# Batch 1's transposes on TensorE, a shorter scale chain and a new instruction order in a fused cross-attention and mixture-of-experts kernel

## The chip, the cores and the metric

The kernel runs on one core of one Trainium2 chip. The metric is device time in microseconds (us), from launch to the last output. The profile adds one recorded execution, whose span runs from its first to its last instruction.

## The reference

There are 8 batches of 512 rows with 256 features (`x`), each with a context of 512 rows of 512 features and a mask of 512 entries. All arithmetic is float32.

```python
# per batch
n   = layernorm(x)                                   # 512 x 256
kv  = (ctx @ W_src.T + b_src) * mask[:, None]        # keys 256, values 256
q   = (n @ W_tgt.T + b_tgt) * mask[:, None]
att = softmax(q k.T / sqrt(32), masked)              # 8 heads of 32
x   = x + concat(n, att @ v) @ W_out.T + b_out
f   = layernorm(x)
w   = top 8 of 16 sigmoid scores of l2norm(f) @ l2norm(gate_w).T, normalized
x   = x + sum_e w[e] * (silu(f @ w_gate[e]) * (f @ w_up[e])) @ w_down[e] + shared expert
```

All 16 experts and the shared one are computed for every row, and a row's 8 unused weights are zero. An expert has a hidden width of 128.

## The kernel before

**Arithmetic.** TensorE multiplies in f16. Every float32 operand is split into a high and a low f16 part, and each product takes three matmuls (`mm3`). ScalarE writes the high part and VectorE or GpSimd the low part by a subtraction. So that the parts keep their digits, operands are scaled by powers of two. For a context that power is found at run time: `attention` takes sums of squares (`junk`, into `cs`), TensorE turns the row maxima (`csT`), a `chain` of VectorE instructions on one element makes the power and its inverse from the exponent's bits, and TensorE spreads both over the partitions (`csB`).

**Stages of a batch.** `attention(b)` loads context, mask and `x`, splits and transposes the context (`ch`) and the normalized `x` (`xh`), projects keys, queries and values (`k`, `q`, `v`), and then runs eight score tiles. A tile covers 4 heads, 128 rows and 512 columns and fills one PSUM buffer, of which there is one (`S=1`). It goes through scores `s` on TensorE, the maximum `nm` on VectorE, four exponentials `p32` on ScalarE, and in two halves through the split `pn` (ScalarE, then GpSimd), a DMA transpose into `pt`, and the product `o` on TensorE. The heads' outputs `on` are transposed (`oh`), projected (`oo`) and added to `x`, once for each half of the batch. `route` normalizes that `x` a second time (`xf`), transposes it (`f`), takes router logits (`lg`) and writes the expert weights to DRAM (`cd`), from where a broadcast load (`cb`) brings each expert's. `ffn` runs 17 experts: `g` and `u` on TensorE, elementwise work on the other three engines, and `y`, in groups of 5, 4, 4 and 4 experts. Batch 0 is routed in two halves, so its `g` and `u` have 256 columns; all others have 512.

**The transposes.** For batch 0, `ctx`, `x`, `o` and the second `x` are transposed on TensorE against the identity into PSUM, as float32, and split from there by ScalarE and VectorE. From batch 1 on, `turn` splits first (names `xm`, `om`, `fm`: ScalarE the high part, GpSimd the low one for `xm` and `om`, VectorE for `fm`) and issues two DMA transposes of 32 tiles each on SyncE's queue; `ch` is done the same way in `cn` with four of 64 tiles. Every `pt` is one of 128 tiles. All other loads and stores are on that queue, too.

**The order.** Nothing is written in a fixed order by hand. `record` lists every operation with a due time `vt`: `attention(b+1)` lies about one batch ahead of `ffn(b)`. `schedule` then plays the list through a table of durations, engine by engine, and emits instructions in the order of the planned starts. Among operations that could start first it takes the one with the lowest due time, no further than `AHEAD` past the oldest open one. `RANK` shifts the due time of each kind of operation and stage by a constant. `SLOTS` says how many buffers each kind of tile has. An engine runs its instructions strictly in that order, so one that waits holds up all that stand behind it.

Of the kernel before, what the change touches and what calls it, by code (L numbers as in the profile page):

```python
# [9 lines left out]
F32 = mybir.dt.float32  # L10
F16 = mybir.dt.float16
# [8 lines left out]
P = 128  # L20
# [11 lines left out]
    x=2, n2=5, cx=4, c16=2, ch=1, xh=1, f=2, qk=4, row=2, mb=1, mx=2, mt=1, p32=2, pn=2, pp=3, v3=2, oc=2, oh=2,  # L32
    cb=3, act=5, hx=6, W=NE + 1, cd=2, mr=1,
# [97 lines left out]
class Plan:  # L131
# [5 lines left out]
    def add(self, eng, dur, calls, port=False, size=0, after=()):  # L137
        outs, ins = [], list(after)
        for _, out, args, kw in calls:
            outs += [o for o in (*out, kw.get("accum_out")) if is_view(o)]  # L140
            ins += [a for a in (*args, *(v for k, v in kw.items() if k != "accum_out")) if is_view(a)]
        name = (outs[0] if isinstance(outs[0], Buf) else outs[0].buf).name
        tag = "".join(c for c in name if not c.isdigit()).strip("_") + eng
        vt = self.vt + RANK.get(tag, {}).get(STAGE.get(self.batch, 2), 0.0)
        op = Op(eng, dur, calls, outs, ins, vt, len(self.ops), port, size)
        op.tag = (self.batch, tag)
        self.ops.append(op)
        return op
# [45 lines left out]
    def dmat(self, tiles, out, in_):  # L194
        self.add("SP", max(1240.0, 16.4 * tiles), [self.call("sync.dma_start_transpose", out, in_)], size=4000 * tiles)

    def dma(self, size, out, in_):
        self.add("SP", 360.0, [self.call("sync.dma_start", out, in_)], size=size)


AHEAD = 1.366
RANK = {
    "aACT": {0: 0.1537, 1: 0.0033, 2: -0.4983, 7: 0.1955},
    "aDVE": {0: 0.0254, 1: 0.2498, 2: -0.2428},
    "aPOOL": {0: -0.0113, 1: 0.6968, 2: 0.5586, 7: 0.0013},
    "amaPE": {-1: 0.2806},
    "ambPE": {-1: 0.1166},
    "bobDVE": {-1: 0.5078},
    "bobSP": {-1: -0.2061},
    "bvbDVE": {-1: 0.105},  # L210
    "cTPE": {0: 0.5508},
    "cbSP": {0: 0.2177, 2: 0.7056, 7: 0.5622},
    "cdSP": {0: 0.0041, 1: -0.029, 2: 0.2104},
    "chACT": {0: -0.6068},
    "chDVE": {0: 0.2153},
    "chSP": {1: 0.0075, 2: -0.8976, 7: -1.0876},
    "cnACT": {1: -0.6307, 2: -0.7293, 7: -0.9914},
    "cnDVE": {1: 0.0087, 2: -0.0023, 7: 0.0346},
    "colsSP": {-1: -0.0672},
    "csBPE": {2: -0.1535, 7: -0.0124},  # L220
    "csTPE": {0: -0.1204, 1: -0.0287, 2: -1.2814, 7: -0.0309},
    "ctACT": {0: 0.864, 1: 0.1003, 2: 0.7227, 7: -0.1018},
    "cxPOOL": {0: 0.6459},
    "cxSP": {-1: 0.0735, 1: 0.0526, 2: -0.9286, 7: -0.0609},
    "fACT": {0: 0.0039},
    "fDVE": {0: 1.0851},
    "fSP": {1: 0.3396, 2: -0.0242, 7: 0.4824},
    "fTPE": {0: 0.3035},
    "fmACT": {1: 0.3782, 2: -0.0974, 7: -0.0187},
    "fmDVE": {2: 0.5311, 7: -0.0959},  # L230
    "fmPE": {-1: -0.1267},
    "fmaPE": {-1: 0.1564},
    "fmbPE": {-1: -0.4319},
    "gPE": {0: 0.1235, 1: 0.207, 2: 0.1559, 7: 0.6056},
    "gTPE": {0: 0.3676, 1: 0.5965, 2: -0.1162, 7: -0.0034},
    "gsqDVE": {-1: -0.4317},
    "gw_nDVE": {-1: -0.1543},
    "gw_nSP": {-1: -2.0117},
    "gwsACT": {-1: 0.0234},
    "gwsDVE": {-1: 0.6316},  # L240
    "hACT": {0: -0.6213, 1: 0.3291, 2: -0.1853, 7: -0.0131},
    "hDVE": {0: 0.1408, 1: 0.0071, 2: -0.2515, 7: -0.0144},
    "hPOOL": {0: -0.3695, 1: 0.2141, 2: -0.0944, 7: 0.3346},
    "junkACT": {1: -0.0113, 2: -0.018, 7: 0.0007},
    "kACT": {0: 0.3565, 1: -0.9183, 2: -0.1216},
    "kDVE": {0: 0.4038, 1: 0.1818, 2: -0.0333, 7: 0.0991},
    "kPE": {0: -0.2174, 1: -0.0614, 2: -0.0344, 7: -1.3012},
    "lgPE": {0: 0.2761, 1: -0.3919, 2: -0.2135, 7: 0.0154},
    "mbSP": {-1: -0.7576, 1: 0.96, 2: 0.035, 7: 0.1462},
    "mcolDVE": {-1: -0.5544},  # L250
    "mkSP": {-1: -0.0456},
    "mkTPE": {-1: -0.2494},
    "mrDVE": {0: 0.88, 1: 0.1094, 2: 0.5668},
    "mvDVE": {0: 0.3115, 1: 0.2223, 2: 0.1576, 7: -0.6709},
    "mwDVE": {1: -0.5933, 2: 0.5831, 7: -0.1328},
    "nmACT": {0: 0.3158, 1: -0.251, 2: -0.0551, 7: -0.0427},
    "nmDVE": {0: 0.0026, 1: 0.0593, 2: -0.1259, 7: -0.1155},
    "oPE": {0: 0.0273, 1: -0.0232, 2: 0.0553, 7: 0.0423},
    "oTPE": {0: 0.1833},
    "ocACT": {0: 0.1024, 1: 0.1925, 2: 0.2005, 7: 0.4061},  # L260
    "ocDVE": {0: 0.1704, 1: -0.1219, 2: -0.6326, 7: -0.0917},
    "ohACT": {0: 0.4072},
    "ohDVE": {0: -0.1733},
    "ohSP": {1: 0.1129, 2: -0.0398, 7: -0.3174},
    "omACT": {2: 0.2922, 7: 0.0002},
    "omPOOL": {1: -0.0603, 2: -0.0508, 7: 0.7467},
    "onPOOL": {0: 0.7499, 1: -0.853, 2: -0.1829, 7: -0.2491},
    "onesPOOL": {-1: -0.3119},
    "ooPE": {0: 0.4931, 1: -0.4365, 2: -0.6844, 7: -0.4352},
    "outSP": {0: 0.4027, 1: -0.3028, 2: 0.4122, 7: 0.4538},  # L270
    "pACT": {0: 0.0182, 1: -0.6748, 2: -0.0234},
    "pnACT": {0: 0.2152, 1: 0.2561, 2: 0.1906, 7: 0.0196},
    "pnPOOL": {0: 0.1635, 1: 0.0141, 2: 0.2234},
    "ptSP": {0: 0.4655, 1: -0.4384, 2: 0.1266, 7: 0.3368},
    "qACT": {0: 0.1257, 1: -0.3375, 2: -0.3996, 7: -0.129},
    "qDVE": {0: -0.2704, 1: -0.4202, 2: -0.5367, 7: -0.2649},
    "qPE": {0: -0.3731, 1: -0.0506, 2: -0.194, 7: -1.1345},
    "qPOOL": {0: -0.0185, 1: 0.126, 7: -0.8731},
    "rDVE": {0: -0.1233, 1: -0.1058, 2: 0.0001, 7: -0.3334},
    "rawSP": {-1: -0.1474},  # L280
    "rhPOOL": {0: -0.1646, 1: -0.4627, 2: 0.6826, 7: 0.2987},
    "riDVE": {0: -0.198, 1: 0.6361, 2: 0.1284, 7: -0.0834},
    "sPE": {1: 0.0314, 2: -0.3686, 7: -0.8384},
    "scACT": {0: -0.0831, 1: 0.4518, 2: -0.1934, 7: -0.1498},
    "scDVE": {0: 0.3459, 1: -0.1583, 2: 0.1869, 7: -0.186},
    "scPOOL": {0: -0.0709, 1: 0.1093, 2: -0.1766, 7: 0.0205},
    "smallDVE": {-1: 0.3026, 1: -0.1537, 2: -0.254, 7: -0.5587},
    "smallPOOL": {-1: -0.2347, 0: -0.1282, 1: -0.3163, 2: 0.0089, 7: 0.0576},
    "sqwACT": {-1: -0.5218},
    "sqwPOOL": {-1: -0.1816},  # L290
    "tDVE": {0: 0.0006, 1: -0.5031, 2: 0.36, 7: 0.0922},
    "uDVE": {0: 0.1229, 1: 0.634, 2: -0.239, 7: -0.259},
    "uPE": {0: -0.1486, 1: 0.6035, 2: 0.715},
    "vACT": {0: 0.2058, 1: 0.1873, 2: -0.0086, 7: 0.1161},
    "vDVE": {0: 0.3577, 1: 0.1322, 2: -0.9791, 7: -0.0565},
    "vPE": {0: 1.1408, 1: -1.3367, 2: -0.1245, 7: 0.2457},
    "vPOOL": {0: -0.0824, 1: -0.3013, 2: -0.4353, 7: 0.59},
    "veDVE": {0: 0.124, 1: -0.0703, 2: -0.0253, 7: -1.3962},
    "vfDVE": {0: 0.0546, 1: -0.7051, 2: 0.0069, 7: 0.2438},
    "wACT": {-1: -0.1553},  # L300
    "wDVE": {-1: -0.0168},
    "wmaPE": {-1: -0.2382},
    "wmbPE": {-1: -0.7302},
    "woACT": {-1: -0.6539},
    "woDVE": {-1: 0.1164},
    "woTPE": {-1: 0.5609},
    "wo_nSP": {-1: 0.2082},
    "wsACT": {-1: -0.3273},
    "wsDVE": {-1: -0.0925},
    "wsTPE": {-1: 0.9299},  # L310
    "ws_naSP": {-1: -0.9149},
    "ws_nbSP": {-1: 0.0231},
    "wtACT": {-1: 0.4585},
    "wtDVE": {-1: 0.4299},
    "wtTPE": {-1: -0.4778},
    "wt_nSP": {-1: 0.0823},
    "xDVE": {0: 0.124, 1: 0.2257, 2: -0.3319, 7: 0.1379},
    "xPOOL": {0: -0.0121, 1: 0.02, 2: 0.1123, 7: -0.199},
    "xSP": {0: 1.1008, 1: 0.0058, 2: 0.0641, 7: 0.353},
    "xTPE": {0: 0.4516},  # L320
    "xfACT": {0: -0.1806, 1: 0.1451, 2: -0.1422, 7: -0.437},
    "xhDVE": {0: 0.6081},
    "xhSP": {1: 0.2024, 2: -0.7682, 7: 0.2589},
    "xmACT": {1: 0.1813, 2: 0.1954},
    "xmPOOL": {1: -0.0234, 2: 0.0256, 7: 0.0077},
    "xnACT": {0: 0.0363, 1: -0.1228, 2: 0.2161, 7: -0.0338},
    "xnSP": {-1: -4.4201, 1: -0.3353, 2: -0.0611, 7: -0.0009},
    "xoPE": {0: -0.2204, 1: -0.0378, 2: -0.3262, 7: -0.1335},
    "yPE": {0: 0.3541, 2: 0.148, 7: 0.1762},
# [7 lines left out]
SAME = {"PE": 0.0, "ACT": 20.0, "DVE": 20.0, "POOL": 20.0}  # L337


def schedule(ops):  # L340
# [9 lines left out]
    port = 0.0  # L350

# [33 lines left out]
    while done < len(ops):  # L385
# [21 lines left out]
        op.start, op.end = st, st + op.dur  # L407
# [694 lines left out]
```

## Time and profile before

| | us |
|---|---|
| median of 3 runs | 959.8 |
| the runs | 959.8, 959.16, 963.09 |
| profiled execution, time | 962.42 |
| profiled execution, span | 960.3 |
| TensorE busy | 860.6 (90%) |
| VectorE, ScalarE, GpSimd busy | 668.5, 654.2, 680.4 |
| mean granted TensorE clock | 0.972 |

The profiled execution is 2.6 us over the median, and 2.1 us of its time lie outside the span. The page gives busy time by engine, then a strip of 40 slices of 24 us, then groups of instructions with the idle time just before them and what ended it. The names in a group are the tile names above without their numbers. Nearly all instructions come from one line, so they are told apart by tile.

### The profile page before, as it was taken

What the parts mean: (1) busy time and instruction counts of PE and PEld (TensorE: products, weight loads), DVE (VectorE), ACT (ScalarE), POOL (GpSimd) and SP (SyncE); (2) the same over time, 40 slices, a digit from 0 to 9 for tenths busy, and PEclk for the clock granted to TensorE, in tenths of its full rate; (3) what the DMA queues carried; (4) which work ended last, traced back from release to release, by engine and by line L of the source; (5) the groups of instructions that cost most, each with busy time, mean ns of one, the idle gap of its engine ahead of it and who ended that gap; (6) DMA issues with size and microseconds to landing.
All of it is one profiled execution on the core that took longest, in us unless ns stands there. A gap on an engine that the chain in (4) does not pass through costs nothing.

```text
span 960.3 us, 21139 instructions
## 1 busy us (share of the span) xinstructions
PE 860.6 (90%) x8007; PEld 547.0 (57%) x8007; DVE 668.5 (70%) x1311; ACT 654.2 (68%) x1133; POOL 680.4 (71%) x830
## 2 busy tenths in 40 slices
PE   3874768989789998989999999989999999999997
PEld 2452446766555565636655556646555666565655
DVE  6666778855876677757785688757886687567554
ACT  3588887874877687757786587757787777534231
POOL 4577778876768787677858786787848976853432
PEclk9886999999889999999999999999999999999999
DMA  8868787798699967999599977998499968951411
GB/s 254 271 124 175 138 157 130 151 197 162 121 205 184 201 133 139 211 191 178 104 198 182 197 145 137 204 191 181 88 189 197 178 110 144 214 120 26 123 56 44
DMA packets 395542, 152.43 MB, mean 159 GB/s; under 512 B 347008, under 2 KB 375216, under 8 KB 395440
## 3 DMA queue, kind: packets, MB, share of 16 engines
q1 hardware_dynamic: 395440, 151.08, 77.9%
q8 instruction: 63, 1.03, 0.5%
q14 instruction: 39, 0.32, 0.2%
HBM read 61.12 MB, written 4.46 MB: 68 GB/s over the span
## 4 chain that ended last, share of the span: by engine, by line
PE 55%; DMA 12%; ACT 11%; DVE 8%; POOL 5%; issue 3%; SPq 1%; POOLq 0%; ACTq 0%; DVEq 0%
PE y L1071 14%; PE u L1071 13%; PE g L1071 12%; DMA pt<-pn 8%; PE s L1071 4%; ACT p L1071 3%; PE o L1071 3%; POOL pn L1071 3%; PE v L1071 3%; DVE nm L1071 3%; PE k L1071 2%; ACT pn L1071 2%; DMA cb<-cd 2%; PE oo L1071 2%; SPq L1071 1%
## 5 line engine op out<-in xcount | busy, mean ns | idle before, releaser
L1071 POOL TENSOR_TENSOR pn<-p,pn 128x1024 f16<-128x1024 f32 x128 | 274.6, 2151 | 57.8 <-ACT pn L1071 48.7
L1071 PEld LDWEIGHTS <-w 128*128 128x128 f16 x1836 | 172.1, 98 | 172.1 <-issue 19.3
L1071 POOL TENSOR_TENSOR a<-a,cb 128x512 f32<-128x512 f32 (+1 forms) x144 | 166.1, 1165 | 73.5 <-DVE a L1071 34.6
L1071 ACT ACTIVATE p<-s,nm,small 128x512 f32<-128x512 f32 x256 | 192.3, 782 | 10.6 <-POOL pn L1071 8.1
L1071 PE MATMUL g<-f,w 128*128 128x512 f16 (+1 forms) x918 | 194.7, 357 | 3.7 <-DVE oc L1071 1.3
L1071 PE MATMUL u<-f,w 128*128 128x512 f16 (+1 forms) x918 | 194.1, 358 | 1.6 <-DVE a L1071 1.6
L1071 PE MATMUL y<-w,h 128*128 128x256 f16 x1632 | 185.9, 273 | 5.6 <-DVE h L1071 4.1
L1071 PEld LDWEIGHTS <-h 128*128 128x128 f16 x1632 | 158.5, 98 | 32.0 <-DVE h L1071 6.7
L1071 ACT CAST pn<-p 128x1024 f16<-128x1024 f32 x128 | 134.5, 1053 | 60.8 <-DMA pt<-pn 60.7
L1071 DVE TENSOR_REDUCE nm<-s 128x4 f32<-128x2048 f32 x64 | 146.2, 2285 | 14.7 <-PE s L1071 14.6
L1071 ACT ACTIVATE a<-g,small 128x512 f32<-128x512 f32 (+1 forms) x153 | 98.1, 645 | 51.7 <-PE g L1071 49.8
L1071 DVE SCALAR_TENSOR_TENSOR a<-a,g 128x512 f32<-128x512 f32 (+1 forms) x153 | 94.5, 622 | 39.1 <-ACT a L1071 38.0
L1071 ACT CAST h<-u 128x512 f16<-128x512 f32 (+1 forms) x117 | 62.8, 540 | 51.0 <-DVE u L1071 49.2
L1071 PEld LDWEIGHTS <-pt 128*128 128x128 f16 x2048 | 69.8, 97 | 36.8 <-DMA pt<-pn 16.5
L1071 DVE TENSOR_TENSOR h<-u,h 128x512 f16<-128x512 f32 (+1 forms) x117 | 72.6, 625 | 25.7 <-ACT h L1071 24.1
L1071 DVE SCALAR_TENSOR_TENSOR x<-y,small,x 128x512 f32<-128x512 f32 x64 | 47.8, 748 | 60.9 <-PE y L1071 60.6
L1071 DVE TENSOR_TENSOR u<-u,a 128x512 f32<-128x512 f32 (+1 forms) x108 | 68.4, 635 | 27.5 <-PE u L1071 22.7
L1071 PE MATMUL o<-v,pt 128*128 128x65 f16 (+1 forms) x2048 | 74.2, 187 | 13.5 <-DMA pt<-pn 10.9
L1071 PE MATMUL s<-k,q 32*128 32x512 f16 x768 | 56.1, 396 | 21.2 <-ACT p L1071 20.7
L1071 POOL TENSOR_TENSOR on<-oc,r 128x128 f32<-128x128 f32 x64 | 30.1, 472 | 31.9 <-DVE oc L1071 20.1
L1071 POOL TENSOR_TENSOR h<-a,h 128x512 f16<-128x512 f32 (+1 forms) x36 | 40.3, 1120 | 15.2 <-ACT h L1071 14.9
L1071 PE MATMUL k<-ch,ws 128*128 128x512 f16 x192 | 45.6, 390 | 5.4 <-DMA ch<-cn 4.1
(188 smaller groups left out, 1055.8 us busy)
## 6 DMA issues: line engine op xcount, KB each, us to landing
cb<-cd SPq DMA_DIRECT2D x112, 256.0 KB, 3.9
cx<-in_ctx_dram SPq DMA_DIRECT2D x32, 256.0 KB, 3.6
xn<-in_x_dram SPq DMA_DIRECT2D x16, 256.0 KB, 3.4
x<-in_x_dram SPq DMA_DIRECT2D x8, 512.0 KB, 4.3
cb<-cd SPq DMA_DIRECT2D x32, 128.0 KB, 3.5
out_dram<-x SPq DMA_DIRECT2D x16, 256.0 KB, 3.1
mb<-in_mask_BxS_fk_dram SPq DMA_DIRECT2D x8, 256.0 KB, 4.6
raw<-in_L_ffn_w_gate_dram SPq DMA_DIRECT2D x16, 128.0 KB, 3.3
```

Source lines behind the costliest of these rows:

```text
L1071: getattr(getattr(nc, eng), m)(*[real(v) for v in (*out, *args_)], **{k: real(v) for k, v in kw.items()})
```

## The change

- `x`, `o` and the second `x` of batch 1 are transposed on TensorE, as those of batch 0 are; `turn` serves them from batch 2 on. The context of batch 1 stays with the DMA transposes. In `route`, the transposes now cover four chunks of rows (two `xf` tiles).
- The chain for a context's scale has four instructions after the reduction in place of seven. One multiply and one lower bound move into the constant `cf2`.
- The planner's model: a DMA transpose is charged 6137 bytes a tile at 272 bytes/ns instead of 4000 at 250 and starts its transfer at its own lead; later DMA issues are held back behind transposes; TensorE work is stretched to twice its length where a model of its clock says so (`Clock`). `AHEAD` and every entry of `RANK` have new values.
- Buffers: `pn` and `oc` have three instead of two, `act` six instead of five, `row` and `oh` one instead of two, `W` 17 instead of 18. The last expert's raw weights are loaded into a `pn` buffer for their squares, and a second time into a `pn` buffer when they are split.

```diff
-    x=2, n2=5, cx=4, c16=2, ch=1, xh=1, f=2, qk=4, row=2, mb=1, mx=2, mt=1, p32=2, pn=2, pp=3, v3=2, oc=2, oh=2,
-    cb=3, act=5, hx=6, W=NE + 1, cd=2, mr=1,
+    x=2, n2=5, cx=4, c16=2, ch=1, xh=1, f=2, qk=4, row=1, mb=1, mx=2, mt=1, p32=2, pn=3, pp=3, v3=2, oc=3, oh=1,
+    cb=3, act=6, hx=6, W=NE, cd=2, mr=1,
...
     def dmat(self, tiles, out, in_):
-        self.add("SP", max(1240.0, 16.4 * tiles), [...], size=4000 * tiles)
+        self.add("SP", max(1240.0, 16.4 * tiles), [...], size=6137 * tiles, lead=650.0 - 4.7 * tiles)
...
-AHEAD = 1.366
+AHEAD = 1.42618182031
 RANK = {
...
+HALFWIN, COLD, HOT = 1706.5, 0.49, 0.82
+class Clock:
+    def run(self, t, work):
+        while True:
+            while self.w < int(t / HALFWIN):
+                f = (self.busy + self.before) / (2 * HALFWIN)
+                self.cold = f <= HOT if self.cold else f < COLD
+                self.before, self.busy = self.busy, 0.0
+                self.w += 1
+            end, r = (self.w + 1) * HALFWIN, 2.0 if self.cold else 1.0
...
-        op.start, op.end = st, st + op.dur
+        op.start, op.end = st, clock.run(st, op.dur) if e == "PE" else st + op.dur
...
         if e == "SP":
-            dma_free = max(dma_free, op.end + 900.0) + op.size / 250.0
+            dma_free = max(dma_free, st + op.lead) + op.size / 272.0
             op.end = dma_free
+            if op.lead < 950.0:
+                free[e] = max(free[e], dma_free - 900.0)
...
+        raw = raws[e] = load_raw(e, "W" if n + 1 < NE else "pn")
...
+        if n + 1 == NE:
+            raw = load_raw(e, "pn")
...
-        chain = [tt(f2[:, 0:1], f2[:, 0:1], cf2[:1], ALU.max),
-                 ts(ex[:, 0:1], ex[:, 0:1], 23, None, ALU.logical_shift_right), ts(ex[:, 0:1], ex[:, 0:1], 20, 125, ALU.max, ALU.add),
-                 ts(ex[:, 0:1], ex[:, 0:1], 1, None, ALU.logical_shift_right), ts(ex[:, 1:2], ex[:, 0:1], 3, None, ALU.subtract),
-                 ts(ex[:, 0:1], ex[:, 0:1], -1, 257, ALU.mult, ALU.add), ts(ex, ex, 23, None, ALU.logical_shift_left)]
+        chain = [stt(f2[:, 0:1], f2[:, 0:1], 2.0, cf2[:1], ALU.mult, ALU.max),
+                 ts(ex[:, 0:1], ex[:, 0:1], 24, 23, ALU.logical_shift_right, ALU.logical_shift_left),
+                 ts(ex[:, 1:2], ex[:, 0:1], 1, 59 << 23, ALU.mult, ALU.add), ts(ex[:, 0:1], ex[:, 0:1], -1, 195 << 23, ALU.mult, ALU.add)]
...
         for k in range(2):
-            if b == 0:
+            if b < 2:
                 t = ps(f"xT{b}{k}")
...
-            if b:
+            if b > 1:
                 turn(on, oh, 0, f"om{b}{hf}", p.pool)
...
-            if b:
+            if b > 1:
                 turn(xf, f, c, f"fm{b}{c}")
-        for k in range(0 if b else 2):
+        for k in range(0 if b > 1 else 2):
             t = ps(f"fT{i}{k}")
-            p.pe(*[p.tr(..., xf[:, c, k * P : (k + 1) * P], ident) for c in range(n)], after=[f[:, :, k, :]])
+            p.pe(*[p.tr(..., xfs[c // 2][:, c % 2, k * P : (k + 1) * P], ident) for c in range(n)], after=[f[:, :, k, :]])
```

## The prediction

> **What bounds the kernel.** I read the strip of 40 slices first, and then the table of busy time by stretches.
>
> ```profile
> span 960.3 us, 21139 instructions
> PE   3874768989789998989999999989999999999997
> PEclk9886999999889999999999999999999999999999
> DMA  8868787798699967999599977998499968951411
> ```
>
> ```profile
> 48.00:72.00 24.00, 18.70 (x244) 13.35 (x241) 16.07 (x48) 19.92 (x33) 18.76 (x16) 0.82 0.67 124
> 72.00:96.00 24.00, 10.09 (x121) 6.65 (x122) 14.96 (x17) 19.98 (x31) 18.21 (x26) 0.64 0.85 175
> 240.00:264.00 24.00, 18.02 (x220) 13.16 (x218) 19.35 (x45) 20.44 (x39) 17.77 (x30) 0.87 0.66 120
> 264.00:288.00 24.00, 20.55 (x199) 12.06 (x199) 16.93 (x44) 18.46 (x33) 16.69 (x29) 0.84 1.08 206
> 576.00:600.00 24.00, 23.16 (x215) 15.51 (x212) 20.47 (x43) 17.70 (x31) 15.22 (x28) 1.00 0.70 134
> ```
>
> The second column is TensorE's busy time, the third last its granted clock. After 336 us TensorE is busy and at full clock almost throughout; before that it waits, and then runs slowly too (0.64 to 0.87). ScalarE is the busiest engine at 72 to 96 us.
>
> To place the loss I use a lag: the time at which a score tile starts, less the TensorE work that stands ahead of it in the order at full clock. The rates are from steady rows: 12 `u` matmuls of 512 columns in 2.60 us (0.217 each), 48 `y` matmuls of 256 columns in 5.24 (0.109), one score tile 0.97, 16 `o` matmuls 0.44, one transpose 0.11. The lag is 26.1 us at the first tile, 64.6 at batch 1's first, 81.0 at its fifth and 82.5 at its last, 89.5 at batch 2's first, 90.1 and 103.7 at its third and fifth, 107.8 at batch 3's first and 135.8 at the last of all. All TensorE work sums to 818 us. Of some 142 us lost, 108 lie before 325 us. The chain of waits and TensorE's timeline show what makes up the middle:
>
> ```profile
> 205.70 7.04 DMA ch<-cn
> 212.79 4.45 PE k L1071 x12
> ...
> 264.12 3.62 DMA f<-fm
> 267.79 0.33 PE lg L1071 x6
> 268.11 2.57 PE g L1071 x6
> ```
>
> ```profile
> 257.87 0.57 PE L1071 MATMUL csB<-small,ones 1*128 1x2 f32 x2 [2.80 <-DVE small L1071]
> 259.77 1.47 PE L1071 MATMUL s<-k,q 32*128 32x512 f16 x12 [1.32 <-ACT p L1071]
> 263.45 0.33 PE L1071 MATMUL lg<-gws,f 128*128 128x16 f16 x6 [0.20 <-DMA f<-fm]
> 267.27 0.33 PE L1071 MATMUL lg<-gws,f 128*128 128x16 f16 x6 [3.49 <-DMA f<-fm]
> ```
>
> A bracket is idle time and who ended it. TensorE waits for batch 1's `f` through the DMA queue, for batch 2's scale, and for batch 2's `ch`; after each wait matmuls take twice as long (12 of 512 columns 4.45 us, 6 take 2.57).
>
> **Part by part**, against the profiled execution's 962.4 us.
>
> *f of batch 1.* The four SyncE transposes and the `fm` step go; two groups of four TensorE transposes and a split from PSUM come. Its waits cost 0.20 + 3.49 + 0.18 = 3.9 us and the slow clock behind them 2.57 - 1.30 and, in `xo`, 1.81 - 1.31: 5.6 in all. In the new order 12.1 us of TensorE work lie between batch 1's last `oo` and `lg` (10.5 before). The last `xf` ended 11.9 us after that `oo`; then come transposes 0.44, cast 0.59, subtraction 0.69 and again some of these, about 2.5. The chain of 14.4 leaves a wait of 2.3. Gain 3.3; bounds 0 and 5.6.
>
> *The scale chain.* Before, one two-input instruction (0.53 us) and six one-input ones (1.03); now one and three: 0.5 less per batch, and only where TensorE waits for it. For batch 3, 4.0 us of work now stand between `csT` and `csB`, where 0.4 did; the chain took 3.5 (254.37 to 257.87). The wait of 2.80, the 1.32 behind it, and the slow score tile (1.92 for 0.97) go: gain 5.1. For batch 2 the work between falls from 2.9 to 0.4, and a chain of 3.0 shows: cost 2.0. The other batches have 2.6 or more and stay at nothing.
>
> *ch of batch 2.* Before, its last DMA transpose was issued behind `pt` tiles that fill SyncE's queue, and `k` waited 2.47 us and ran 4.45 - 2.60 = 1.85 too long. In the new order all four stand ahead of a `pt` whose `o` comes before that `k` on TensorE, so that `k` has nothing of its own to wait for. Gain 4.3; bounds 0 (the wait moves to that `o`) and 7.0, the lag's growth there.
>
> *FFN work drawn ahead.* Up to batch 1's fifth tile ScalarE sets the pace (21.4 us busy in 96 to 120). By mean rows its work ahead of that tile is 134.4 us now and 132.7 before; TensorE's is 94.8 and 87.1. If ScalarE keeps its pace, 7.7 - 1.7 = 6.0 us of lag are gone; bounds 0 and 10.
>
> *Transposes and their cover.* 24 of 0.11 us: 2.6 on TensorE, 5.2 at half clock. Four subtractions of 1.16 us leave GpSimd; `xh` and `oh` add four of 0.69 to VectorE, and `f` saves two of 0.25, 2.3 us that its idle time hides (3.8 of 24 us at 144 to 168); with that gone they cost 2.3. SyncE loses 12 issues of 1.24 to 1.67 us, 15 to 20 us of queue, which stood before the `pt` of batch 0's late tiles and of batch 2's first. Beyond `f` and `ch` I take 1.5, between 0 and 3.
>
> [...] The transposes of `pt` hold SyncE's queue 2.97 us for 512 KB each when it is full (221.43 and 228.63 us), 177 GB/s, while plain loads filled the second slice with 271. [...] On the other side, TensorE's transposes of `oT` at 142 us start 0.11 apart. [...]
>
> *Edits at nothing.* The second load of one expert (three issues of 0.43 us on SyncE, beside batch 0's first `cb`) hides behind the wait of GpSimd's `a`; uncovered it is 1.3. The third `pn` buffer answers the largest wait of ScalarE:
>
> ```profile
> L1071 ACT CAST pn<-p 128x1024 f16<-128x1024 f32 x128 | 134.5, 1053 | 60.8 <-DMA pt<-pn 60.7
> ```
>
> But 60.1 of it lie after 170 us, where TensorE has other work; its own waits for `pt` after 336 us sum to 10.3. Nothing, bound 10 gained. One `row` and one `oh` buffer: TensorE holds their next writers apart by several matmul groups; nothing, bound 3 lost. The start does source weights and `v` first: 18.5 us of TensorE work stand before the first score tile (13.8 before), but 25.9 and 24.6 before the third, so it evens out; bounds 6 lost and 4 gained. Batches 3 to 7, where the lag grows by 28.0 us: nothing taken, bounds below.
>
> Sum: 3.3 + 5.1 - 2.0 + 4.3 + 6.0 - 2.6 + 1.5 = 15.6 us. 962.4 - 15.6 = 946.8 in a profiled execution, and 2.6 less in the median: 944.
>
> **Rivals.**
>
> *Slower: the router waits in the later batches.* For batches 3, 4, 5 and 7 the TensorE work between the last `oo` and `lg` falls from 28.7, 28.7, 30.0 and 22.2 us to 15.1, 15.1, 14.9 and 13.0, and these keep their DMA transposes.
>
> ```profile
> 350.87 1.47 PE L1071 MATMUL oo<-wo,oh 128*128 128x256 f16 x12
> 361.51 2.06 ACT L1071 ACTIVATE xf<-x,small,vf 128x256 f32<-128x256 f32 x4
> 369.30 5.68 SPq L1071 DMA_TRANSPOSE f<-fm  x4
> 377.44 0.75 PE L1071 MATMUL lg<-gws,f 128*128 128x16 f16 x24
> ```
>
> In batch 2 that took 25.1 us (352.3 to 377.4). For it: TensorE would stall in order, with everything behind `lg`. Against it: only about 16 are needed in a row (6.9 to the bias, by 352.4 to 358.7 and two GpSimd steps; 1.1 first `xf` pair, 1.5 split, 5.0 of issue, 1.3 landing), and the rest was queueing behind work with nearer use. At 16 the four stalls sum to 6; at 18.5 they come to 16 and take back the whole gain, from where it is slower; at 25 they cost 42. Time 960 to 986. Chance 0.17.
>
> *No change: the front is paced elsewhere.* ScalarE's work before batch 2's fifth tile is 207.1 us after and 208.1 before. If attention arrives no sooner and FFN work doesn't fill its gaps, only the scale's and `ch`'s waits go, and the transposes are paid: 959.8 - 5.1 + 2.0 - 4.3 + 2.6 = 955, with 2 to 5 more if `o` takes over the wait for `ch`. 954 to 961. Chance 0.13.
>
> *More: the third `pn` and less queueing carry on.* The waits for `pt` after 336 us (10.3) and half of the lag's other growth there go too: 944 - 12 = 932, range 922 to 934. Chance 0.17.
>
> **How the numbers follow.** The forecast has 0.53, with 934 to 954 as its own range. The range of 924 to 966 leaves out a little of the top case and about half of the slow one. A measurement of this kernel tells 0.5% from no change, 955.0 to 964.6. Faster: 0.53 + 0.17 + 0.04 of the no-change case = 0.74. Same: 0.09 + 0.02 of the slow one's low end = 0.11. Slower: 0.15.
>
> **What would show it.** Right: no wait of `lg` over 3 us at batch 1, `csB` of batch 3 and `k` of batch 2 without idle time ahead of them, clock slices near 264 us at 9, and a lag of about 75 at batch 1's fifth tile and 88 at batch 2's fifth. Wrong: a wait at `lg` of 4 us or more in batches 3 to 5, a first score tile after 46 us, or lag growing by more than 28 from batch 3 on.

## The result and the profile after

The changed kernel took 967.5 us (median of 6 runs, 965.4 to 968.7) beside 960.7 for the kernel before (6 runs). The ratio is 1.0062, 95% interval 1.0041 to 1.0084: slower by 0.6%. The forecast was 944. The profiled execution took 965.4, its span 963.7.

The strip of the page of after:

```profile
span 963.7 us, 21105 instructions
...
PE   3944878899899999999899998999998999998997
...
PEclk8956899899999999999999999999999999999999
DMA  8868667798698968996599947997699839982411
```

Slices 11 and 12 (241 to 289 us) went from 7 and 8 to 8 and 9 and their clock from 8 to 9, as forecast. But the third slice fell from 7 to 4, and from 458 us on four slices stand at 8 where one did. The table of busy time by stretches of after (TensorE's busy time second, granted clock third from the end):

```profile
48.00:72.00 24.00, 10.84 (x176) 6.94 (x175) 11.68 (x21) 19.83 (x35) 20.86 (x13) 0.58 0.62 132
72.00:96.00 24.00, 9.65 (x126) 6.22 (x127) 17.01 (x30) 16.74 (x25) 14.91 (x29) 0.64 0.85 154
240.00:264.00 24.00, 20.88 (x250) 16.15 (x249) 19.00 (x47) 21.30 (x42) 18.59 (x30) 1.00 0.61 130
264.00:288.00 24.00, 22.32 (x220) 12.94 (x219) 18.78 (x44) 19.80 (x35) 16.51 (x22) 0.93 0.99 184
576.00:600.00 24.00, 19.78 (x202) 11.88 (x199) 18.21 (x49) 19.88 (x37) 12.38 (x16) 1.00 0.69 138
```

ScalarE, which was to keep its pace at the start, is busy 16.74 us of 24 at 72 to 96 us where it was 19.98, and TensorE at 576 to 600 us lost 3.4 us. The three waits on which the forecast's gain rested are gone, as TensorE's timeline of after shows:

```profile
213.25 2.75 PE L1110 MATMUL k<-ch,ws 128*128 128x512 f16 x12
...
261.71 0.28 PE L1110 MATMUL csB<-small,ones 1*128 1x2 f32 x2
...
265.33 0.23 PE L1110 MATMUL lg<-gws,f 128*128 128x16 f16 x3 [0.97 <-DVE f L1110]
265.93 0.68 PE L1110 MATMUL lg<-gws,f 128*128 128x16 f16 x21 [0.36 <-DVE f L1110]
```

The lag, counted as in the prediction, says where it was lost. Its growth in each stretch, in us, with two kernels told of below (n_before and n_after, two of those in the next table):

| stretch | before | forecast | after | n_before | n_after |
|---|---|---|---|---|---|
| start to batch 0's fourth tile | 38.8 | 38.8 | 38.6 | 39.7 | 37.9 |
| to batch 1's fifth tile | 42.2 | 36.2 | 49.5 | 45.6 | 44.6 |
| to batch 3's first | 26.8 | 16.1 | 14.3 | 24.8 | 10.7 |
| to batch 7's last | 28.0 | 28.0 | 31.9 | 20.1 | 15.6 |
| to the end | 6.6 | 6.6 | 8.9 | 5.1 | 6.1 |
| TensorE's work | 817.9 | 820.5 | 820.5 | 817.9 | 820.5 |
| span | 960.3 | 944.7 | 963.7 | 953.2 | 935.4 |

(The forecast's column leaves 1.5 us for SyncE unplaced, which stands in its span.) The middle came out better than forecast. The second stretch missed by 13.3 us and the last two by 6.2.

### The profile page after: what moved, and what is told of

Same layout as the page of the kernel before. It is cut to its first block, busy times and chain, and to the rows that moved or that the text cites. A ratio compares the mean times of both kernels' runs of the same rounds, so it can differ in the third digit from the quotient of the medians.

```text
span 963.7 us, 21105 instructions
## 1 busy us (share of the span) xinstructions
PE 863.9 (90%) x8031; PEld 550.1 (57%) x8031; DVE 676.8 (70%) x1292; ACT 652.1 (68%) x1133; POOL 667.2 (69%) x826
## 4 chain that ended last, share of the span: by engine, by line
PE 51%; ACT 12%; DMA 12%; POOL 10%; DVE 10%; issue 5%; SPq 1%; ACTq 0%; POOLq 0%; DVEq 0%
PE y L1110 12%; PE u L1110 11%; PE g L1110 10%; DMA pt<-pn 5%; ACT p L1110 4%; POOL pn L1110 4%; PE s L1110 4%; PE o L1110 3%; DVE nm L1110 3%; PE v L1110 3%; PE k L1110 2%; POOL a L1110 2%; ACT pn L1110 2%; PE oo L1110 2%; PE xo L1110 1%
## 5 line engine op out<-in xcount | busy, mean ns | idle before, releaser
L1110 PE MATMUL g<-f,w 128*128 128x512 f16 (+1 forms) x918 | 198.9, 360 | 7.2 <-DVE h L1110 3.6
L1110 PE MATMUL y<-w,h 128*128 128x256 f16 x1632 | 190.0, 275 | 4.9 <-DVE h L1110 4.6
L1110 DVE SCALAR_TENSOR_TENSOR a<-a,g 128x512 f32<-128x512 f32 (+1 forms) x153 | 94.1, 622 | 42.7 <-ACT a L1110 42.2
L1110 PE MATMUL o<-v,pt 128*128 128x65 f16 (+1 forms) x2048 | 77.7, 188 | 24.6 <-DMA pt<-pn 22.8
L1110 ACT ACTIVATE nm<-nm,small 128x4 f32<-128x4 f32 x64 | 24.8, 388 | 64.3 <-DVE nm L1110 63.9
L1110 POOL TENSOR_TENSOR h<-a,h 128x512 f16<-128x512 f32 (+1 forms) x36 | 38.6, 1072 | 21.3 <-ACT h L1110 21.3
L1110 PE MATMUL v<-ws,ch 128*128 128x256 f16 x384 | 46.5, 280 | 0.3 <-DVE a L1110 0.3
```

The costliest lines, as they stand in the source:

```text
L1110: getattr(getattr(nc, eng), m)(*[real(v) for v in (*out, *args_)], **{k: real(v) for k, v in kw.items()})
```

## Two theories

*Theory 1:* the edits gain what they were made for, and the new order of instructions, that is the values of `AHEAD` and `RANK`, eats it. *Theory 2:* the edits themselves cost (TensorE's transposes with their splits, one `W`, `row` and `oh` buffer less), in any order.

Two kinds of kernels tell them apart. Some keep an order and change the code: the planner plans with one kernel's operations, and those of the variant are then emitted in that sequence.

```diff
-    ops = schedule(record(io))
+    ops = pinned(record, io)    # sequence from schedule() with the first code, operations from the second
```

The others get other values of `AHEAD` and `RANK` for the code, from a search that minimizes the planner's own planned end. Each kernel ran beside the kernel before, whose median lay between 960.2 and 963.6 us from one series to the next, so kernels are to be compared by the ratios.

| kernel | code | order | us | ratio to before, interval |
|---|---|---|---|---|
| b_pin | before | before | 963.4 | 0.9999 (0.9976 to 1.0022) |
| b_newchain | + short chain | before | 958.5 | 0.9953 (0.9933 to 0.9973) |
| b_tr | + transposes | before | 962.4 | 1.0011 (0.9991 to 1.0030) |
| b_both | + both | before | 959.6 | 0.9954 (0.9931 to 0.9976) |
| a_pin | after | after | 968.3 | 1.0076 (1.0050 to 1.0101) |
| a_oldchain | - short chain | after | 969.2 | 1.0074 (1.0051 to 1.0096) |
| a_notr | - transposes | after | 987.2 | 1.0252 (1.0225 to 1.0279) |
| n_before | before, new planner | searched | 953.8 | 0.9922 (0.9897 to 0.9947) |
| n_oldplan | after, old planner | searched | 968.5 | 1.0074 (1.0044 to 1.0104) |
| n_after2 | after | searched | 960.0 | 0.9977 (0.9956 to 0.9997) |
| n_after | after | searched | 938.5 | 0.9766 (0.9740 to 0.9793) |
| n_pin | after | that of n_after | 943.0 | 0.9786 (0.9756 to 0.9816) |
| n_oldchain | - short chain | that of n_after | 948.3 | 0.9848 (0.9815 to 0.9881) |

## Experiments: the edits in a kept order

Emitting in a kept sequence deals equal buffers out afresh, so the unchanged kernels were run in this form too, as b_pin and a_pin.

> The kernel before, every instruction in its own order; only which of equal buffers (PSUM banks, act) a tile gets is dealt out afresh, as in the runs with one edit. Theory 1 (the short chain is what gained in b_newchain): ratio 0.998 to 1.002. Rival (the dealing of banks gained it): 0.993 to 0.997.

> The changed kernel, every instruction in its own order; only which of equal buffers (pn, act) a tile gets is dealt out afresh. All theories: as the changed kernel, ratio to before 1.004 to 1.008; what it differs by is the price of that dealing, and is taken off the runs made in the same way.

b_pin is level with before and a_pin lies with the changed kernel. The dealing is no cause that these runs can tell.

**The short chain in the old order.** b_newchain is before's order with the four instructions of the change's diff.

> The kernel before with its own order, but the scale's chain of four instructions instead of seven. Theory 1: 0.5 us less in each batch and TensorE waited for it 9.9 us in six, so 1 to 3 us faster, ratio 0.997 to 0.999, the wait of csB in batch 2 about 2.3 instead of 2.80. Theory 2: no gain, ratio 1.000.

It was faster by 0.5%, some 4 us and more than expected. The wait of 2.80 us fell to 2.27, but all waits of TensorE's matmuls at `csB` for VectorE fell only from 4.8 to 3.5 us (the 9.9 us in the expectation count the idle time of the weight loads too). Where the rest arises was not traced. The wait of 2.80 is batch 3's; the expectation and the prediction's opening call it batch 2's, the prediction's sum has it right.

**The transposes in the old order.** In b_tr `b == 0` becomes `b < 2` in the three places of the diff; the added steps stand directly behind what they read.

> The kernel before with its own order of every instruction, but batch 1's x, o and second x transposed on TensorE as in the change (the steps that this adds stand directly behind what they read). Theory 1 (the edits gain, the new order eats it): faster than before by 4 to 10 us, ratio 0.990 to 0.996; the lag's growth from batch 2's first score tile to its fifth falls from 13.6 (89.5 to 103.7, less 0.6) to about 7, and lg of batch 1 waits under 1 us. Theory 2 (the edits themselves cost): 962 or more, ratio 1.000 to 1.006, with the lag at batch 2's fifth tile still over 100 us.

A miss: no difference. The local part came, smaller than expected (the lag's growth from batch 2's first score tile to its fifth, 14.2 before, was 10.0, and the lag at batch 3's first tile 103.0 for 107.8), but 2.6 us of TensorE work were added and 2.3 us of the gain were given back by batch 7.

> The kernel before with its own order, with both edits at once: batch 1's x, o and second x transposed on TensorE, and the scale's chain of four instructions. Theory 1 (the edits gain what the two runs alone showed, and the new order is what eats it): about the sum of the two ratios, 0.994 to 0.998, so 955 to 958 us, with the lag at batch 3's first score tile about 101 (107.8 before, 103.0 and 105.1 with one edit each). Theory 2 (the edits take the gain from each other): 0.999 to 1.003.

Both together gave what the chain gave alone. In the old order the two edits are worth 0.5% and cost nothing, which speaks against theory 2. The buffers are those of before in these kernels, and no run changes them alone.

**The edits taken out of the new order.**

```diff
-        chain = [stt(f2...), ts(ex...), ts(ex...), ts(ex...)]          # a_oldchain
+        chain = [tt(f2...), ts(ex...), ts(ex...), ts(ex...), ts(ex...), ts(ex...), ts(ex...)]
-            if b > 1: turn(on, oh, ...)                                # a_notr; likewise xh and f
+            if b: turn(on, oh, ...)
```

> The changed kernel with its own order, but the old chain of seven instructions. Theory 1 (the place in the order decides, not the chain's length): the csB waits of 3.31 us in batches 5 and 6 grow by about 0.5 each, and the whole by 1 to 4 us: ratio to before 1.007 to 1.010. Theory 2 (the short chain itself costs): at or below the changed kernel, 1.003 to 1.006.

> The changed kernel with its own order, but batch 1's x, o and second x transposed by SyncE's DMAs again as before (the steps that come back stand directly behind what they read). Theory 1: the waits return, of lg of batch 1 by 4 to 8 us and at xo and oo of batch 1, less 2.6 us of TensorE's transposes: 3 to 10 us slower than the changed kernel, ratio to before 1.009 to 1.017. Theory 2 (the transposes themselves are the cost): 0.998 to 1.004.

The waits of 3.31 us at `csB` in batches 5 and 6 grew to 3.86, as expected, but the time by less than could be told: a_oldchain is level with a_pin. The DMA transposes cost 1.7% against a_pin (1.0252 to 1.0076, some 17 us), more than expected. TensorE's timeline of a_notr:

```profile
275.40 0.33 PE L1192 MATMUL lg<-gws,f 128*128 128x16 f16 x6 [3.53 <-DMA f<-fm]
...
280.44 0.33 PE L1192 MATMUL lg<-gws,f 128*128 128x16 f16 x6 [3.45 <-DMA f<-fm]
```

Between 184 and 340 us TensorE's waits of `lg` for `f` sum to 8.9 us and those of `oo` for `oh` to 4.8. The rest was not traced, and a part may be the place of the steps that came back, put by hand into an order laid out without them. As placed here, the transposes are worth nothing in the one order and 1.7% in the other: what an edit is worth belongs to the order.

## Experiments: another order for the same edits

```diff
-AHEAD = 1.42618182031
+AHEAD = 1.621858
...
-    "csBPE": {0: 0.4147, 1: 0.0276, 2: -0.453, 7: -0.0822},
-    "csTPE": {0: 0.712, 1: 0.012, 7: 0.4638},
+    "csBPE": {0: 0.7807, 1: -1.3106, 2: -1.4906, 7: -0.938},
+    "csTPE": {0: -0.6625, 1: -1.0967, 2: -0.7041, 7: -0.652},
```

(n_after; all values of `RANK` differ.)

> The changed kernel with all its edits, buffers and planner, but other constants of the order (AHEAD and RANK), for which the kernel's own planner ends at 922 us instead of 944. Theory 1 (the order that the change brought is what costs): the chip runs some 20 us over the plan, as it did with the changed kernel (963.7 for 944.4), so a span near 942 to 950, ratio to before 0.978 to 0.990. Theory 2 (buffers and edits cost in any order): no faster than before, 0.998 to 1.006.

> As n_after, with a second set of constants found from the change's own ones, planned end 929 us. Theory 1: about 7 us behind n_after, 948 to 957, ratio 0.985 to 0.997. Theory 2: as n_after, 0.998 to 1.006.

> The kernel before with its own edits undone nowhere (DMA transposes in batch 1, seven-instruction chain, old buffers), but planned with the changed planner, which knows TensorE's clock and the DMA queue, and with constants for which that planner ends at 929 us. Theory 1 (the order decides, and the edits are worth some 5 us): faster than before, 948 to 956, ratio 0.986 to 0.996, and slower than n_after by 5 to 10 us. Rival (the new planner gives no better order than the old one): 0.997 to 1.004.

> The changed kernel's edits and buffers, but planned with the old planner, without clock and with its old queue, and with constants for which that one ends at 927 us (it ended at 925 for the kernel before, which took 960.3). If the planner's knowledge of clock and queue is what makes a plan hold on the chip: some 33 us over the plan, 958 to 964, ratio 0.997 to 1.005. If only the edits matter: 0.994 to 0.997, as both edits gave in the old order.

n_after took 938.5 us, 2.3% less than before and 3% less than the changed kernel, with every edit and buffer of the change. This rules out theory 2, by which the edits and buffers cost in any order: with the same code, the order alone makes 29 us. That the edits gain in every order it does not show, as n_oldplan and n_after2 below do not bear that out. The strip of n_after:

```profile
span 935.4 us, 21112 instructions
...
PE   2775777899999999989999999999999999999997
...
PEclk9976988999999999999999999999999999999999
```

From 187 us on, only one slice before the last stands below 9. TensorE's waits from 200 us on, in all us, times and the longest, first of after and then of n_after:

```profile
PE csB L1110 <- DVE small L1110: 6.6, 2, 3.3
PE o L1110 <- DMA pt<-pn: 5.8, 8, 1.2
PE y L1110 <- DVE h L1110: 4.6, 7, 1.0
PE g L1110 <- DVE h L1110: 3.3, 3, 1.7
```

```profile
PE o L1114 <- DMA pt<-pn: 3.7, 7, 1.0
PE s L1114 <- ACT p L1114: 1.3, 2, 1.1
PE y L1114 <- DVE h L1114: 1.1, 2, 0.8
```

These four kinds make 20.3 us in after. In n_after `o` and `y` make 4.8, and `csB` and `g` on `h` are not among the seven largest, of which the last has 0.7. The planner's planned ends, worked out by the kernel's own `schedule`, stand to the spans as follows:

| | planned end | span | over |
|---|---|---|---|
| before, n_oldplan (old model) | 925.0, 927.4 | 960.3, 965.8 | 35, 38 |
| after, n_after, n_after2, n_before (new model) | 944.4, 921.8, 929.2, 929.5 | 963.7, 935.4, 954.3, 953.2 | 19, 14, 25, 24 |

With the new model the chip keeps closer to the plan, in four plans of four. But the plan that the change carries ends 22.6 us later than another that the same model finds for the same code, and on the chip that came to 28.3. n_before (953.8) shows the new model and constants for it to be worth 0.8% without the edits; n_after2, with the edits and a plan of about the same end, was 0.5% slower than that. This is a miss, and shows that a few us of planned end are no measure. n_oldplan missed too: with the edits, the old model and a planned end only 2.4 us behind that of before, it took 0.7% more than before, above both its expectations. So n_after is the best of three searched orders for these edits and not what any search brings, and how much of its gain over n_before (1.6%) belongs to the edits, the buffers or the search is open.

**The chain in the good order.**

> n_after, every instruction in its own order, with buffers dealt out afresh. Theory 1: as n_after, ratio to before 0.974 to 0.980; the dealing is worth less than 3 us.

> n_pin with the old chain of seven instructions. TensorE waited for csB 0.2 us in all in n_after. Theory 1 (0.5 us more per batch is hidden where work stands between csT and csB): within 2 us of n_pin. Rival (the chain is paid on VectorE wherever it stands): 3 to 5 us more, 0.5 in each batch and the slow clock behind it.

n_pin has a ratio of 0.9786 beside 0.9766 for n_after, with intervals that overlap. The old chain in its order cost 5.3 us, the size that the rival named. TensorE waited nowhere for `csB` in n_pin; in n_oldchain the list of waits has

```profile
PE csB L1174 <- DVE small L1174: 3.4, 3, 1.7
```

in batches 1, 5 and 7, so not in each batch as the rival had it; where the other 1.9 us arise was not traced. The lag is kept to the end (114.8 against 120.0 at the last tile).

## Experiments: where in the new order

**Batches 5 and 6.** The timeline of after, TensorE and VectorE:

```profile
465.65 2.75 PE L1110 MATMUL u<-f,w 128*128 128x512 f16 x12
471.71 0.58 PE L1110 MATMUL csB<-small,ones 1*128 1x2 f32 x2 [3.31 <-DVE small L1110]
...
466.05 0.25 DVE L1110 TENSOR_REDUCE small<-csT 1x1 f32<-1x128 f32 x1
...
468.46 0.68 DVE L1110 TENSOR_TENSOR h<-u,h 128x512 f16<-128x512 f32 x1
...
471.02 0.12 DVE L1110 SCALAR_TENSOR_TENSOR small<-small 1x1 f32<-1x1 f32 x1
471.17 0.49 DVE L1110 TENSOR_SCALAR small<-small 1x1 int32<-1x1 int32 x3
...
476.39 0.75 DVE L1110 SCALAR_TENSOR_TENSOR x<-y,small,x 128x512 f32<-128x512 f32 x1 [3.85 <-PE y L1110]
```

The chain is 0.6 us of work, but 4.7 us of statistics and FFN steps stand between its reduction and its first instruction. Two kernels move this: a_chainup puts the chain directly behind the reduction, and a_stats moves in batches 5 and 6 also the statistics into the idle time behind.

```diff
+        at[chain] = directly behind the reduction of csT       # a_chainup: batches 1 to 7; a_stats: 5 and 6
+        at[bn_stats, bn_aggr] = directly behind csB's copy     # a_stats
```

> The changed kernel with its own order, but the scale's chain moved on VectorE to stand directly behind its reduction in batches 1 to 7 (in batches 5 and 6 about 5 us of normalisation statistics stood between). Theory 1: the csB waits of 3.31 us in batches 5 and 6 go, and with the slow clock behind them 5 to 8 us: ratio to before 0.997 to 1.002. Theory 2: the wait turns into one for what was moved behind the chain, ratio 1.004 to 1.008.

> As a_pin, but in batches 5 and 6 three batch-norm statistics and three aggregates (1.8 us of VectorE, needed 30 us later) stand behind csB's copy, in a stretch where VectorE idles 2.3 to 3.9 us, and the scale's chain directly behind its reduction. Theory 1a (VectorE's pile-up ahead of csB is a loss of the order): the 3.31 us that TensorE waits there falls to 1.5 or less in each, and the whole by 3 to 5 us, ratio to a_pin 0.995 to 0.997. Rival (lag won there is lost again before the end): within 1 us of a_pin.

Both missed. a_chainup took 974.3 (ratio 1.0127, interval 1.0095 to 1.0160), slower than a_pin by some 5 us with intervals that just touch, of which its profile, of an execution of 968.7, shows little; a_stats 965.7 (1.0069, 1.0046 to 1.0093), not to be told from a_pin. In both kernels TensorE waits 2.06 + 1.42 us at the same place, where it had waited 3.31. The timeline of a_stats, TensorE, VectorE and GpSimd in turn, shows why:

```profile
471.89 0.38 PE L1172 MATMUL csB<-small,ones 1*128 1x2 f32 x2 [2.06 <-DVE h L1172]
473.68 2.62 PE L1172 MATMUL y<-w,h 128*128 128x256 f16 x14 [1.42 <-DVE h L1172]
...
467.75 0.66 DVE L1172 SCALAR_TENSOR_TENSOR small<-small 1x1 f32<-1x1 f32 x1
468.45 0.49 DVE L1172 TENSOR_SCALAR small<-small 1x1 int32<-1x1 int32 x3
469.01 1.62 DVE L1172 TENSOR_TENSOR fm<-xf,fm 128x512 f16<-128x512 f32 x1
...
471.16 0.68 DVE L1172 TENSOR_TENSOR h<-u,h 128x512 f16<-128x512 f32 x1
...
465.89 2.52 POOL L1172 TENSOR_TENSOR a<-a,cb 128x512 f32<-128x512 f32 x2 [0.34 <-DVE small L1172]
468.93 1.16 POOL L1172 TENSOR_TENSOR h<-a,h 128x512 f16<-128x512 f32 x1 [0.53 <-ACT h L1172]
```

The scale was ready at 468.94, but `csB` began at 471.89, when VectorE's `h` ended. By the kernel's own dealing of buffers, `csB` writes into one of the four PSUM buffers (`P=4`) that an expert's `u` holds until this `h` has read it. In after the same `h` ended at 469.14, 3.1 us after the reduction began, and so before the scale. With the chain in front of it, it ended 4.4 us after the reduction began, in both kernels, and `csB` waited for it instead. In a_stats, the statistics gone, VectorE's steps fell beside those of GpSimd: the chain's first instruction took 0.66 instead of 0.12 and ended with GpSimd's `a` at 468.41, and `fm` took 1.62 instead of 0.66 and ended 0.54 behind GpSimd's `h`.

**The start.** The timeline of after at batch 0's sixth score tile:

```profile
78.17 4.21 POOL L1110 TENSOR_TENSOR pn<-p,pn 128x1024 f16<-128x1024 f32 x2
...
80.69 2.23 DVE L1110 SCALAR_TENSOR_TENSOR cn<-cx,small,cn 128x512 f16<-128x512 f32 x1
...
83.88 2.88 DVE L1110 SCALAR_TENSOR_TENSOR w<-raw16W,small,w 128x768 f16<-128x768 f32 x1
...
84.81 0.85 PE L1110 MATMUL o<-v,pt 128*128 128x65 f16 x16 [6.99 <-DMA pt<-pn]
...
86.79 0.93 ACT L1110 ACTIVATE w<-raw0W,small 128x768 f16<-128x768 f32 x1 [3.26 <-DVE w L1110]
...
91.15 1.47 PE L1110 MATMUL s<-k,q 32*128 32x512 f16 x12 [5.50 <-ACT p L1110]
```

ScalarE's exponentials, for which TensorE waits, stand behind a weight step that waits 3.26 us for VectorE, whose `cn` and `w` beside GpSimd's `pn` took 2.23 and 2.88 us; the next of each took 0.74 and 1.02. a_front moves the weight steps 0 to 3 behind these exponentials.

> As a_pin, but the expert weights' steps 0 to 3 on ScalarE and VectorE (raw0 to raw3, from 86.8 us) stand behind the exponentials of batch 0's sixth score tile, so that ScalarE does not wait 3.26 us for VectorE ahead of them. Theory 1b (this wait is the start's loss): that tile starts 3 to 5 us sooner than 91.15 us, and the lag at batch 1's first tile falls from 71.3 to 67 to 69; ratio to a_pin 0.995 to 0.998. Rival (the start is bound by pt and GpSimd's pn, and the tile behind waits instead): the lag at batch 1's first tile stays at 70 to 72, and the time within 1 us.

> a_stats and a_front in one. Theories 1a and 1b: the sum of both, 5 to 9 us less than a_pin, about level with the kernel before (0.997 to 1.001). Rivals: 1.004 to 1.008.

a_front took 967.4 (1.0075, 1.0050 to 1.0100), level with a_pin, and the lag at batch 1's first tile was 73.5 for 73.7: the rival. But this is no test of the 3.26 us: in a_pin, which has the order of after, the wait at this place was short.

```profile
87.76 0.94 ACT L1160 ACTIVATE w<-raw0W,small 128x768 f16<-128x768 f32 x1 [0.94 <-DVE w L1160]
```

The lag still grew from batch 0's fourth tile to batch 1's fifth within half a us of after's growth, so the 3.26 us do not make up the loss. ScalarE's steps in a_front waited for something else:

```profile
86.30 0.72 ACT L1162 ACTIVATE cn<-cx,small 128x512 f16<-128x512 f32 x1 [2.57 <-DMA ch<-cn]
...
89.29 0.72 ACT L1162 ACTIVATE cn<-cx,small 128x512 f16<-128x512 f32 x1 [1.60 <-DMA ch<-cn]
```

that is, for SyncE's queue. a_two took 972.2 (1.0130, 1.0105 to 1.0156), slower than either; which wait makes this up was not found. Moving steps by hand repaired none of the places. What was shown is that the order as a whole costs; that a certain step of it does was not.

## Why the prediction was wrong, by its steps

- *f of batch 1, scale of batch 3, ch of batch 2:* right. `lg` waits 1.3 us (2.3 forecast), batch 3's `csB` and batch 2's `k` not at all, and the stretch to batch 3 grew by 14.3 for 16.1. The 2.0 us taken off for batch 2's scale were too much: its `csB` waited 0.6 us, and 0.4 before.
- *FFN work drawn ahead:* the step that failed. It took ScalarE's work as the pace and 6.0 us as gained; the stretch lost 7.3 (49.5 for 42.2, where 36.2 was forecast), and the lag at batch 1's fifth tile was 88.1 where 75 was named as a sign of being right. The stretch from batch 0's fourth tile to batch 1's fifth by windows, then TensorE's longest waits in it, before and after:

```profile
67.20:168.04 100.84, 69.18 (x798) 48.35 (x799) 75.29 (x149) 83.70 (x144) 78.87 (x108) 0.88 0.80 148
67.07:182.98 115.91, 82.42 (x865) 57.21 (x864) 85.79 (x174) 90.02 (x161) 81.35 (x117) 0.83 0.72 135
```

```profile
PE s L1071 <- ACT p L1071: 17.8, 5, 7.0
...
PE o L1110 <- DMA pt<-pn: 16.6, 8, 7.0
PE s L1110 <- ACT p L1110: 6.1, 2, 5.5
```

  ScalarE (the fourth busy time) was idle 17.1 us in before and 25.9 in after. TensorE had waited mostly for ScalarE's exponentials (`p`); now it waited mostly for `pt`. So ScalarE no longer set the pace. What made `pt` late was not found, and no kernel here, n_after included, has this stretch under the 42.2 of before. A busy engine's work is a lower bound of when a tile comes, not its time.
- *"The other batches have 2.6 or more and stay at nothing":* failed. In batches 5 and 6, 2.75 us of TensorE work stood between `csT` and `csB`, but from the reduction's start to the chain's end VectorE's queue took 5.6 us, not the 0.6 of the chain's instructions. What these two waits cost in the end is not shown, as a_chainup and a_stats only turned them into waits for `h`. n_oldchain shows the other side: 0.5 us of chain a batch cost 5.3.
- *Batches 3 to 7 at nothing:* failed by 3.9 us and 2.3 in the tail. The sign that the prediction named for this (lag growing by more than 28) came. The new waits are those listed above for after; which of them make it up was not shown.
- *The third `pn`:* taken at nothing, and no run changes it alone, so its worth is open. The group's wait in after:

```profile
L1110 ACT CAST pn<-p 128x1024 f16<-128x1024 f32 x128 | 134.3, 1058 | 3.3 <-DMA pt<-pn 2.4
```

  60.8 us of ScalarE's idle time became 3.3, and TensorE's waits for `pt` after 336 us fell from 10.3 to 3.9 us, but the time did not follow.
- *Transposes at 2.6* was right in TensorE's work (in after four `oT` of batch 1 took 0.60 us at 200.91 us and started 0.11 apart), *the start evens out* too (38.6 for 38.8 at batch 0's fourth tile). The 1.5 us for SyncE no run shows; in the old order `f`, `ch`, the transposes and SyncE, 6.5 us of the sum, gave nothing together (b_tr).
- *Rival "no change: the front is paced elsewhere":* right in that attention arrived no sooner. It took the front as level, though, and the front lost 7.3 us.
- *Rival of the router waits:* the sign (slower) was right and the mechanism wrong. `lg` waits for `f`'s DMA once after batch 2, 1.0 us in batch 7.
- What no step weighed is the order's length as a whole. Each wait of before was priced by whether it would go, and the new order's own waits at nothing, where the profile of before cannot show them. The size of the forecast was reached by the same edits in n_after, but not by its terms: the stretch above grew by 44.6 us there, and the gain lies behind it (10.7 and 15.6 us for 26.8 and 28.0).

## What to carry to other kernels

When a change brings new constants for a planner, separate them: run the new code in the old order, and search the order again for the new code, before the code is judged. A wait removed by hand in this dense order came back a step later (3.31 us became 2.06 + 1.42). Price a chain by what its engine has queued between its first and last step, not by its instructions, and ask what else its consumer waits for, here a PSUM buffer.

## What the runs showed of the hardware

In the rows shown, steps of VectorE that began during GpSimd's long ones took longer and ended shortly behind them. In after a `cn` took 2.23 us and ended 0.54 behind `pn`; at 88.69 us, with GpSimd idle, one took 0.75. In a_front a step of 128x1 took 1.78 us, from 81.26 to 83.04, and `pn` ended at 83.02; in after at 83.14 us, with GpSimd idle, such a step took 0.16:

```profile
78.37 4.65 POOL L1162 TENSOR_TENSOR pn<-p,pn 128x1024 f16<-128x1024 f32 x2
...
81.26 1.78 DVE L1162 TENSOR_TENSOR small<-small 128x1 f32<-128x1 f32 x1
```

What makes them longer was not shown. The planner keeps such steps apart in time, but only in its plan, and the six spans above ended 14 to 38 us behind it.

The same order, with buffers dealt out afresh, also started differently: the lag at batch 0's fourth tile was 38.8 in before and 35.6 in b_pin. A difference of 3 us there is no evidence for an edit.
